# A fixed timetable of seven streams per group, and a residual kept without its mean

## The chip, the cores and the metric

The kernel runs on one core of one Trainium2 chip. The metric is the device time of one execution in microseconds; of several executions the median counts. Five engines work side by side, each through a queue of its own in order: PE (matrix products; PEld is its loading of the stationary operand), DVE and POOL (elementwise work), ACT (functions and copies), and SP, which issues DMAs.

## The reference

128 graphs of 128 nodes with 64 features pass through four layers; each normalises, takes the ReLU, and adds its result to x.

```
h = relu(layernorm(x)); x = x + L0(h, adj)     # 192 hidden values per edge
h = relu(layernorm(x)); x = x + L1(h, adj)     # three graph convolutions, 128 wide
h = relu(layernorm(x)); x = x + L2(h, adj)     # product, row norm, batch norm over all nodes
h = relu(layernorm(x)); x = x + L3(h, adj)     # tanh
L0: mask = adj > 0
    e[j,k] = relu(h[j] @ W1a + (h[j] - h[k]) @ W1b + b1)
    out[j] = sum_k mask[j,k] * e[j,k] @ W2 + deg[j] * b2
L1: three times relu(adj @ (h @ W + b)), then @ Wout + bout, times the node mask
L2: y = ((adj @ h + h) @ W + b); y /= max(|y|, 1e-12)
    mean and variance of y over all nodes of all graphs; relu(affine(y)) * mask
L3: tanh([h, adj @ h] @ W1 + b1) @ W2 + b2
layernorm(x) = (x - mean) / sqrt(var + 1e-5), over the 64 features
```

About one eighth of adj's entries are not zero, so layer 0 need not visit every pair of nodes.

## The kernel before

The 128 graphs form NG = 32 groups of G = 4. Up to the batch norm of layer 2 a group passes through on its own; layer 3 follows for all groups once that norm's mean and variance are known.

**Layer 0 per group.** `prepare` (L406) loads and transposes adj, ranks each node's neighbours with products against triangular matrices (ps_rank, ps_rankT), sorts the nodes by degree (key, lower, ps_place, to_b), and numbers the neighbours (num). It normalises x (layernorm_relu, L316), projects it (ps_q, L468 and L469 copy it) and splits the projection q into three bf16 parts, and it computes the node's own part (ps_p, psort). q and num go to DRAM and come back as near_q and near_n, laid out in thirds of the nodes. A group then has 20 tasks (ORDER, L46): 12 "near" ones and 8 others. For each task ACT fills a PSUM block with psort (`fill`, L563), DVE compares num with a constant to pick one neighbour per node (`make_onehot`, ohn L544 for three tasks at once, oh L549), PE adds the picked q with 4 or 12 matrix products of 128x192 (`differences`, L565), and DVE adds the ReLU of the block to a sum (acc, L582 the first, L586 the others; one per group is made by ACT, L584). There are three blocks, so a block's next fill waits for its accumulation. `layer0_end` (L589) undoes the sort with products (ps_sA, ps_sB), applies W2 and adds to x.

**Layers 1 and 2 per group.** `layer1` (L615) and `layer2_norm` (L648) are chains of product, PSUM copy, product. Every normalisation has on DVE a mean (L303), a subtraction (L304), a sum of squares (L309), a reciprocal (L323) and h (L313), and on ACT a square (L307) and a square root (L321). `layer2_norm` also adds y into column sums that stay in spare PSUM columns (`add_sums`), with the weights as the stationary operand; `total` (L683) picks the own graph's entries and sums.

**What sets the order.** The kernel is recorded group by group. Beside the tasks of group g run two generators, `prepare(g+1)` and `after_layer0(g-1)`. At every half task a budget of estimated PE time (`spent`, PACE, L105 and L748 to L767) decides how many of their steps are recorded. A step often holds several operations of several engines. The framework's scheduler then orders each engine's queue by its own estimates of when operands are ready; it may move instructions against the recorded order.

**The end.** After the last group's layer 2, y loses a first estimate of the mean (shift, L791, made from groups 0 to 29), is squared (L793) and summed. The affine constants follow (L806 to L810). Then the groups pass in parts of 1, 3, 4, 6, 6, 6, 6: `normed` (L833) makes the new x of a group (two operations on POOL, except group 0's, which DVE does; then DVE, with statistics by L845), `roots` (L847) makes the scales of a whole part with a square root on ACT (L857), and `layer3_h`, `layer3_gather`, `layer3_tanh` and `layer3_end` (L865 to L903) make the output. `layer3_gather` brings h into transposed form by a product with the identity (L883).

Of the kernel before, what the change touches and what calls it, by code (L numbers as in the profile page):

```python
# [18 lines left out]
P = 128  # L19
# [28 lines left out]
FIRST, FIRST_R = 0, ORDER.index((None, FULL))  # L48
N_PREPARE, N_AFTER = 14, 26
PACE, LAG = 0.85, 2.5  # L50
LATE = 14
LASTS = 1.9
PARTS = [1, 3, 4, 6, 6, 6, 6]
AHEAD = 3
# [19 lines left out]

def network(ctx, tc, io, out, over=None, x1=None):

    nc = tc.nc  # L80
# [13 lines left out]
    ps = ctx.enter_context(tc.tile_pool(name="ps", bufs=8 - 2 * NBLK, space=PSUM))  # L94

    xs = [keep.tile([P, G, F], F32, tag=f"x{g}", name=f"x{g}") for g in range(NG)]
# [8 lines left out]
    spent = {"us": 0.0, "kind": None}  # L105

    def spend(w, n, dtype):
        f32 = dtype == F32
        kind = (f32, tuple(w.shape), n)
        m = w.shape[-1]  # L110
        one = max(0.026, 0.00043 * n) if not f32 else max(0.22, 0.0018 * n) * (0.5 if m == F and n == P else 1.0)
        spent["us"] += one + (0.045 if kind != spent["kind"] else 0.0)
        spent["kind"] = kind

    def matmul(o, w, x, **kw):
        spend(w, math.prod(x.shape[1:]), x.dtype)
        return nc.tensor.matmul(o, w, x, **kw)  # L117

    def transpose(o, x, i):
        spent["us"] += 0.115  # L120
        spent["kind"] = None
        return nc.tensor.transpose(o, x, i)


    ident = keep.tile([P, P], F32, name="ident")
    make_identity(nc, ident)
    ident_b = keep.tile([P, P], BF16, name="ident_b")
    nc.vector.tensor_copy(ident_b, ident)
# [8 lines left out]
    row = once.tile([P, G, F], F32, tag="db", name="row").rearrange("p b f -> p (b f)")[:, 0:P]  # L137
    nc.gpsimd.iota(row, [[1, P]], base=0, channel_multiplier=0, allow_small_or_imprecise_dtypes=True)
    row_b = keep.tile([P, P], BF16, name="row_b")
    nc.vector.tensor_copy(row_b, row)  # L140
# [21 lines left out]
    nc.gpsimd.memset(order_row, 0.0)  # L162
# [3 lines left out]
    nc.vector.memset(caps[:, 0:1], float(3 * NEAR + FULL))  # L166
    nc.vector.memset(caps[:, 1:2], float(FULL))
    for n in SEGS:
        in_n = work.tile([P, G], F32, tag="mean", name="in_n")[:, 0:1]
        nc.vector.tensor_scalar(in_n, neg_p[:, 0:1], float(-n), float(BLOCKS), ALU.is_gt, ALU.mult)  # L170
        nc.vector.tensor_tensor(caps, caps, in_n.to_broadcast([P, 2]), ALU.add)
# [13 lines left out]
    nc.vector.tensor_scalar(wq, wp, -1.0, None, ALU.mult)  # L185
    nc.vector.tensor_tensor(wp, wp, wtop, ALU.add)
    w2a = keep.tile([P, F], F32, name="w2a")
    nc.sync.dma_start(w2a, w2[0:P, :])
    def blockdiag(name, w, width):

        t = keep.tile([P, 2, width], F32, name=name)
        nc.gpsimd.memset(t, 0.0)
        nc.sync.dma_start(t[0:F, 0, :], w)
        nc.sync.dma_start(t[F:P, 1, :], w)
        return t

    w2b = blockdiag("w2b", w2[P:H0, :], F)
# [14 lines left out]
    gout = load("gout", [P, F], io["L1_gnn_Wout"])  # L212
# [6 lines left out]
    total_n = sum(s.shape[0] for _, ss in parts for s in ss)  # L219
    cat = once.tile([P, NP, W], F32, tag="acc1", name="cat").rearrange("p a n -> p (a n)")[0:3, 0:total_n]  # L220
    where, at = {}, 0
    for name, srcs in parts:
        first = at
        for s in srcs:
            nc.sync.dma_start(cat[:, at : at + s.shape[0]], s.rearrange("(o n) -> o n", o=1).broadcast_to([3, s.shape[0]]))
            at += s.shape[0]
        where[name] = slice(first, at)
    rows3 = keep.tile([P, total_n], BF16, name="rows3")
    nc.gpsimd.memset(rows3, 0.0)

    def split_biases():

        c = ohn.tile([P, 3, G, P], BF16, tag="ohn", name="c3").rearrange("p t b n -> p (t b n)")[0:3, 0:total_n]
        for q in range(3):
            nc.vector.tensor_copy(c, cat)
            if q == 0:
                nc.vector.tensor_scalar(rows3[0:3], c, ident[0:3, 0:1], None, ALU.mult)
            else:
                nc.vector.scalar_tensor_tensor(rows3[0:3], c, ident[0:3, q : q + 1], rows3[0:3], ALU.mult, ALU.add)
            yield  # L240
            if q < 2:
                nc.vector.tensor_tensor(cat, cat, c, ALU.subtract)
                yield

# [11 lines left out]
    b2_all = bias_all("b2_all", io["L0_gnn_b2"])  # L256
# [12 lines left out]
    ysum, ysq = (t.rearrange("p (a n) -> p a n", a=2)[0:G, :, W:512] for t in blks[0:2])  # L269
# [3 lines left out]


    nm_in = once.tile([P, G, P], F32, tag="to", name="nm_in")[:, 0]
    nc.scalar.dma_start(nm_in, nodemask)
    nm = keep.tile([P, P], F32, name="nm")
    pt = ps.tile([P, 512], F32, tag="ps", name="ps_nm")
    transpose(pt[:, 0:P], nm_in, ident)
    nc.vector.tensor_copy(nm, pt[:, 0:P])  # L280

# [10 lines left out]
    def bank(name):  # L292
        return ps.tile([P, 512], F32, tag="ps", name=name)
# [6 lines left out]
    def center(xt, xc, var, tag=""):  # L300

        mean = work.tile([P, G], F32, tag="mean" + tag, name="mean")
        nc.vector.tensor_reduce(mean, xt, AX.X, ALU.add)  # L303
        nc.vector.scalar_tensor_tensor(xc, over_f(mean), -1.0 / F, xt, ALU.mult, ALU.add)  # L304
        yield
        sq = (once if tag else work).tile([P, G, F], F32, tag="sq" + tag, name="sq")
        nc.scalar.activation(sq, xc, AF.Square)  # L307
        yield
        nc.vector.tensor_reduce(var, sq, AX.X, ALU.add)  # L309

# [5 lines left out]
    def layernorm_relu(xt, tag="", h=None):  # L316
        xc = (once if tag else work).tile([P, G, F], F32, tag="xc" + tag, name="xc")
        var = work.tile([P, G], F32, tag="var" + tag, name="var")
        yield from center(xt, xc, var, tag)
# [5 lines left out]
        yield 2  # L325
        return h

    def transposed(h, tag="", pt=None):

        pt = bank("ps_hT") if pt is None else pt  # L330
        for p in range(NP):
            transpose(pt[:, p * P : (p + 1) * P], h[:, 2 * p : 2 * p + 2, :].rearrange("p b f -> p (b f)"), ident)
        hT = (once if tag else work).tile([P, NP, P], F32, tag="hT" + tag, name="hT")
        nc.scalar.copy(flat(hT), pt[:, 0 : NP * P])  # L334
        return hT

    def gathered(h, rT, tag, pt=None):

        pt = bank("ps_ga") if pt is None else pt
        for p in range(NP):  # L340
            for k in range(2):
                b = 2 * p + k
                o = pt[k * F : (k + 1) * F, p * P : (p + 1) * P]
                matmul(o, h[:, b, :], rT[:, b, :], start=True, stop=True)
        t = (once if tag == "hs" else work).tile([P, NP, P], F32, tag=tag, name=tag)
        nc.scalar.copy(flat(t), pt[:, 0 : NP * P])
        return t
# [20 lines left out]
    proj, near_q, near_n = [], [], []  # L368
    for i in range(2 if x1 is None else 0):
        proj.append(keep.tile([P, 3, NP, W], BF16, name=f"q{i}"))  # L370
        near_q.append(keep.tile([P, 3, NP, W], BF16, name=f"near_q{i}"))
        near_n.append(keep.tile([P, 3, G, P], BF16, name=f"near_n{i}"))
        for t in (near_q[-1], near_n[-1]):
            nc.gpsimd.memset(t, 0.0)
# [16 lines left out]
    def save_transposed(g, a):  # L391
        adjT = adjTs[g] = adjp.tile([P, G, P], F32, tag="adjT", name="adjT")
        pt = bank("ps_aT")
        for b in range(G):
            transpose(pt[:, b * P : (b + 1) * P], a[:, b, :], ident)
        nc.scalar.copy(flat(adjT), pt)
        nc.sync.dma_start(saved[g], flat(adjT))
        return adjT

    sorts, psorts, accs = {}, {}, {}  # L400

    def load_group(g):
        nc.sync.dma_start(xs[g], x[g * G : (g + 1) * G].rearrange("b n f -> n b f"))
        loaded[g] = load_adj(g)

    def prepare(g):  # L406

        xt, parts_q = xs[g], proj[g % 2]
# [3 lines left out]

        adjT = save_transposed(g, a)
        mT = once.tile([P, G, P], BF16, tag="mT", name="mT")
        yield
        nc.vector.tensor_scalar(mT, adjT, 0.0, None, ALU.is_gt)
        ln = layernorm_relu(xt, "0")
        next(ln)
        yield
# [4 lines left out]
        pk = bank("ps_rankT")  # L424
        matmul(pk, upto_t, flat(mT), start=True, stop=True)
        leftT = once.tile([P, G, P], BF16, tag="leftT", name="leftT")
        nc.vector.scalar_tensor_tensor(flat(leftT), pk, float(NEAR), flat(mT), ALU.is_gt, ALU.mult)
# [4 lines left out]
        yield  # L432
        pr = bank("ps_rank")
        prv = pr.rearrange("p (b n) -> p b n", n=P)
        for b in range(G):
            matmul(prv[:, b, :], leftT[:, b, :], upto, start=True, stop=True)
        pk = bank("ps_key")
        matmul(pk, ones_b, flat(leftT), start=True, stop=False)
        matmul(pk.rearrange("p (b n) -> p b n", n=P), ones_b, order_row.unsqueeze(1).to_broadcast([P, G, P]), start=False, stop=True)
        key = edge.tile([P, G], F32, tag="key", name="key")  # L440
        nc.vector.tensor_scalar(key, prv[:, :, P - 1], order, None, ALU.add)
        next(ln)
        lower = once.tile([P, G, P], BF16, tag="lower", name="lower")
        nc.vector.tensor_tensor(lower, pk.rearrange("p (b n) -> p b n", n=P), key.unsqueeze(2).to_broadcast([P, G, P]), ALU.is_lt)
        rank = once.tile([P, G, P], BF16, tag="rank", name="rank")
# [645 lines left out]
```

## Time and profile before

| what | us |
|---|---|
| median of 3 runs (1381.01 to 1384.86) | 1383.9 |
| the profiled execution, its time | 1382.45 |
| its span, first to last instruction | 1380.7 |
| PE, DVE, ACT, POOL busy in the span | 1189.1, 1178.6, 986.9, 267.7 |
| accumulations L586, 576 of them | 542.9 on DVE |
| block fills L563, 544 from psort and 96 from psort_r | 436.1 and 78.2 on ACT |
| first and last start of L582, the first accumulation of a group | 45.2 and 1191.7 |

A page of the profile gives each engine's busy time, and groups of equal instructions with their count, busy time, mean time of one in ns, and the idle time of the engine just before them with the instruction that ended most of it. The records name a line, an engine, an operation and the tiles (written <- read). All matrix products of the kernel before carry line 117 or 122, a helper's, so they are told apart by their tiles. "PE blk" is a task's product into a block, whichever task it is. The granted clock of PE is 1.00 in the steady stretch and 0.97 to 0.73 from 1200 to 1300 us.

### The profile page before, as it was taken

How to read it: one execution, taken by the hardware profiler on the slowest of the kernel's cores; microseconds unless marked ns; L12 is line 12 of the kernel's file. 1: busy time of each engine (PE TensorE's matmuls, PEld its weight loads, DVE VectorE, ACT ScalarE, POOL GpSimd, SP SyncE). 2: the span in 40 equal slices, each digit the busy share in tenths (PEclk: the TensorE clock that was granted, in tenths of full speed). 3: DMA queues.
4: the chain of work that ended last, by engine and by line, in shares of the span. 5: the costliest groups of instructions: out<-in, count | busy, mean ns of one | idle time of the engine just before them, and what ended most of it. 6: DMA issues, size and time to landing. Idle time of an engine off the chain costs nothing.

```text
span 1380.7 us, 29280 instructions
## 1 busy us (share of the span) xinstructions
PE 1189.1 (86%) x10968; PEld 961.3 (70%) x10968; DVE 1178.6 (85%) x2643; ACT 986.9 (71%) x1870; POOL 267.7 (19%) x329
## 2 busy tenths in 40 slices
PE   4799888988988888888898988888888888896886
PEld 2577777777777777777777777777777777774665
DVE  7999898889888898898889888889888888874764
ACT  2777777777777777777777777777777777754853
POOL 4111111111111111111111111111111111113652
PEclk8999999999999999999999999999999999998799
DMA  4454222222232232222223333232222222200344
GB/s 119 122 141 113 78 75 67 68 72 84 84 84 84 77 84 73 79 76 72 69 62 84 84 84 85 76 84 76 76 79 72 63 55 71 77 16 15 97 131 107
DMA packets 108787, 110.96 MB, mean 80 GB/s; under 512 B 42895, under 2 KB 88220, under 8 KB 108636
## 3 DMA queue, kind: packets, MB, share of 16 engines
q1 hardware_dynamic: 108172, 108.74, 28.9%
q8 instruction: 88, 1.44, 0.4%
q14 instruction: 63, 0.52, 0.1%
q10 hardware_dynamic: 464, 0.26, 0.1%
HBM read 52.70 MB, written 35.29 MB: 64 GB/s over the span
## 4 chain that ended last, share of the span: by engine, by line
PE 41%; ACT 31%; DVE 20%; issue 4%; DMA 2%; SPq 1%; POOL 0%; DVEq 0%; ACTq 0%
PE blk L117 15%; ACT blk L563 14%; DVE acc L586 8%; PE ps_sA L117 5%; PE ps_pr L117 4%; DVE ohn L544 4%; PE ps_o L117 3%; PE ps_ag L117 3%; ACT extra L528 3%; PE ps_sB L117 3%; PE ps_q L117 2%; ACT q L468 2%; ACT q L470 2%; ACT acc L584 2%; PE ps_hm L117 2%
## 5 line engine op out<-in xcount | busy, mean ns | idle before, releaser
L586 DVE SCALAR_TENSOR_TENSOR acc<-blk,acc 128x768 f32<-128x768 f32 x576 | 542.9, 950 | 92.2 <-PE blk L117 68.4
L563 ACT COPY blk<-psort 128x768 f32<-128x768 f32 x544 | 436.1, 806 | 162.6 <-DVE acc L586 141.5
L117 PE MATMUL blk<-q,oh 128*128 128x192 bf16 x3072 | 324.1, 247 | 28.9 <-ACT blk L563 28.2
L117 PEld LDWEIGHTS <-oh 128*128 128x128 bf16 x3072 | 261.6, 98 | 83.8 <-issue 70.4
L117 PE MATMUL blk<-near_q,ohn 128*128 128x192 bf16 x1536 | 205.5, 247 | 40.8 <-ACT blk L563 28.5
L117 PEld LDWEIGHTS <-ohn 128*128 128x128 bf16 x1536 | 134.4, 98 | 91.3 <-issue 72.9
L544 DVE TENSOR_SCALAR ohn<-near_n 128x1536 bf16<-128x1536 bf16 x128 | 101.9, 838 | 0.0
L471 POOL TENSOR_TENSOR q<-rest,q 128x768 bf16<-128x768 f32 x32 | 52.5, 1642 | 233.9 <-ACT q L470 233.9
L645 POOL TENSOR_TENSOR adjT<-adjT,ident 128x512 f32<-128x512 f32 x32 | 41.8, 1307 | 255.4 <-PE ps_ag L117 255.4
L672 POOL TENSOR_TENSOR y<-y,nrm 128x256 f32<-128x256 f32 x31 | 19.0, 612 | 339.2 <-PE blk L117 305.8
L563 ACT COPY blk<-psort_r 128x768 f32<-128x768 f32 x96 | 78.2, 814 | 0.5 <-DMA fro_r<-fro 0.4
L117 PE MATMUL ps_pr<-g,dT 128*128 128x128 f32 x512 | 71.2, 282 | 5.0 <-ACT dT L629 5.0
L117 PEld LDWEIGHTS ps_pr<-g,dT 128*128 128x128 f32 x512 | 64.5, 191 | 14.0 <-ACT dT L629 13.2
L117 PE MATMUL ps_ag<-adjT,msg 128*128 128x128 f32 x512 | 70.8, 281 | 0.4 <-ACT msg L637 0.4
L117 PEld LDWEIGHTS ps_ag<-adjT,msg 128*128 128x128 f32 x512 | 62.1, 191 | 3.4 <-ACT msg L637 2.8
L629 ACT ACTIVATE dT<-ps_ag 128x512 f32<-128x512 f32 x96 | 56.7, 591 | 6.5 <-PE ps_ag L117 6.5
L117 PE MATMUL ps_q<-wq,hT 128*128 128x384 f32 x128 | 52.2, 531 | 4.6 <-ACT hT L334 0.5
L117 PE MATMUL ps_sA<-fro,acc 128*128 128x128 f32 x256 | 53.3, 290 | 1.3
L637 ACT COPY msg<-ps_pr 128x512 f32<-128x512 f32 x64 | 37.4, 585 | 23.2 <-PE ps_pr L117 23.2
L117 PE MATMUL ps_p<-wp,hs 128*128 128x384 f32 x128 | 51.8, 486 | 0.0
L528 ACT ACTIVATE extra<-psort,spare_n 128x192 f32<-128x192 f32 x128 | 50.4, 453 | 0.1
L117 PE MATMUL ps_sA<-fro_r,acc 128*128 128x128 f32 x256 | 50.1, 277 | 0.0
(226 smaller groups left out, 2493.6 us busy)
## 6 DMA issues: line engine op xcount, KB each, us to landing
q_dram<-q SPq DMA_DIRECT2D x32, 567.0 KB
near_q<-q_dram SPq DMA_DIRECT2D x96, 189.0 KB
near_n<-n_dram SPq DMA_DIRECT2D x96, 126.0 KB
a<-in_adj_dram SPq DMA_DIRECT2D x32, 256.0 KB
adjT_dram<-adjT SPq DMA_DIRECT2D x32, 256.0 KB
adjT<-adjT_dram SPq DMA_DIRECT2D x32, 256.0 KB
psort_r<-psort SPq DMA_DIRECT2D x32, 228.0 KB
fro_r<-fro SPq DMA_DIRECT2D x32, 152.0 KB
```

Of the source, the lines that this page charges most:

```text
L117: return nc.tensor.matmul(o, w, x, **kw)
L468: nc.scalar.copy(parts_q[:, 0, p, :], pq[:, 0:W])
L470: nc.scalar.copy(parts_q[:, 1], rest)
L471: nc.gpsimd.tensor_tensor(parts_q[:, 2], rest, parts_q[:, 1], ALU.subtract)
L528: nc.scalar.activation(of(extra, b), of(psort, b), AF.Relu, scale=spare_n[:, g, b, 0:1])
L544: nc.vector.tensor_scalar(oh.rearrange("p t b n -> p (t b n)"), near_n[g % 2].rearrange("p t b n -> p (t b n)"), float(i + 1), None, ALU.i ...
L563: nc.scalar.copy(columns(t), psorts[g][in_segments(n)])
L584: nc.scalar.activation(acc, o, AF.Relu)
L586: nc.vector.scalar_tensor_tensor(acc, o, 0.0, acc, ALU.max, ALU.add)
L629: nc.scalar.activation(flat(dT), pa, AF.Relu)
L637: nc.scalar.copy(flat(msg), pm)
L645: nc.gpsimd.tensor_tensor(adjT, adjT, ident.unsqueeze(1).to_broadcast([P, G, P]), ALU.add)
```

## The change

All five engines' proxies are wrapped: every instruction that is recorded through them is pinned behind the one recorded before it on its engine. So up to the end stage the recorded order is the order of the queues. The end stage is still left to the scheduler.

```diff
+class InOrder:
+        def call(*args, **kw):
+            ins = op(*args, **kw)
+            if hasattr(ins, "ins"):
+                self.tc.keep_in_program_order(ins)
+            return ins
...
-    nc = tc.nc
+    nc = Engines(tc)
```

The recorded order comes from a timetable. Each group has seven streams: `sort` and `project` (the former prepare), `pick` (one-hots), `fill`, `subtract` (products), `gather` (accumulations) and `after_layer0`. Each is a generator with many short steps, mostly one operation of one engine, and a list of due times, one per step, counted from the group's start; groups start PERIOD = 3491 apart. The step with the earliest due time whose gate is open comes next; a gate asks for a free PSUM bank or for an earlier step. Due times give an order only, nothing on the chip waits for a clock. PSUM banks for side work (2 as before) are now handed out by the kernel. Group 31's streams are paced by 0.75, its last one by 0.4. Group 0 has its tasks in another order, with five that need no near copy first.

```diff
-PACE, LAG = 0.85, 2.5
+ORDERS = {0: OTHERS[:FULL] + [k for k in ORDER if k not in OTHERS[:FULL]]}
+LAST = 0.75, 0.75, 0.4
+PERIOD = 3491
+FILL_PLAN = [-821, -601, -88, -32, 293, 492, 556, 878, 958, 1216, 1216, 1369, ...
+GATHER_PLAN = [-689, -689, -47, 463, 463, 755, 931, 1073, 1306, 1306, 1511, ...
...
+            for stage, plan, start, scale in (
+                (sort, SORT_PLAN, at - PERIOD if g else early, 1.0),
+                (project, PROJECT_PLAN, at - PERIOD if g else early, 1.0),
+                (pick, PICK_PLAN, at, 1.0 if last else LAST[0]),
+                (fill, FILL_PLAN, at, 1.0 if last else LAST[0]),
+                (subtract, SUBTRACT_PLAN, at, 1.0 if last else LAST[0]),
+                (gather, GATHER_PLAN, at, 1.0 if last else LAST[0]),
+                (after_layer0, AFTER_PLAN, at + (PERIOD if last else PERIOD * LAST[0]), (LAST[2], LAST[1], 1.0)[min(last, 2)]),
+            ):
+                streams.append(Stream(stage(g), plan, start, scale))
+        streams.append(Stream(squares(), [0], (NG - 1) * PERIOD))
+        while streams:
+            s = min((s for s in streams if s.gate is None or s.gate()), key=lambda s: s.due())
+            s.step()
```

The residual x is kept without its mean over the features, and the mean in a 65th column. `project` centres x once; what is added later is centred already, since the matrices W2, Wout and the biases b2 and bout are centred during set-up, with their row means in a 65th column. Layers 1 and 2 normalise without a mean and a subtraction. In layer 2 POOL adds the mean back into x.

```diff
-        nc.vector.tensor_reduce(mean, xt, AX.X, ALU.add)
-        nc.vector.scalar_tensor_tensor(xc, over_f(mean), -1.0 / F, xt, ALU.mult, ALU.add)
+    def centre(xm):
+        mean = xm[:, :, F]
+        nc.vector.tensor_reduce(mean, xm[:, :, 0:F], AX.X, ALU.add)
+        yield
+        nc.vector.scalar_tensor_tensor(xm[:, :, 0:F], over_f(mean), -1.0 / F, xm[:, :, 0:F], ALU.mult, ALU.add)
+        nc.vector.tensor_scalar(mean, mean, 1.0 / F, None, ALU.mult)
...
     def layer2_norm(g):
-        h = yield from layernorm_relu(xt)
+        h = yield from norm_relu(xt)
+        nc.gpsimd.tensor_tensor(xt, xt, over_f(xms[g][:, :, F]), ALU.add)
```

The sums of y have y as the stationary operand now, with an eight-column result, and `total` ends in one product. The shift and squares of y become a stream that starts with the last group instead of a loop behind it. In the end stage the transposed h comes from a transpose, and the root of `roots` moves from ACT to POOL.

```diff
-            matmul(sums[:, p, :], weights, t[:, 2 * p : 2 * p + 2, :]..., start=False, stop=True, ...)
+            matmul(sums[:, p, :], t[:, 2 * p : 2 * p + 2, :]..., weights, start=False, stop=True, ...)
...
-            matmul(pt[0:F, n], h[:, b, :], ident, start=True, stop=True)
+            transpose(pt[0:F, n], h[:, b, :], ident)
...
-        nc.scalar.activation(r, r, AF.Sqrt, bias=eps, scale=1.0 / F)
-        nc.vector.reciprocal(r, r)
-        if not late:
+        nc.vector.scalar_tensor_tensor(s0, s1, 1.0 / F, s0, ALU.mult, ALU.add)
+        nc.vector.tensor_scalar(s0, s0, LN_EPS, None, ALU.add)
...
+        if late:
+            nc.gpsimd.tensor_tensor(s0, s0, halves[:, 0 : len(gs), :], ALU.pow)
+            nc.vector.tensor_copy(r, s0)
+        else:
+            nc.gpsimd.tensor_tensor(r, s0, halves[:, 0 : len(gs), :], ALU.pow)
```

In set-up, two casts move from DVE to ACT, the clearing of near_q and near_n from POOL to DVE, the table of capacities from DVE to POOL, and the splitting of the biases is cut in two parts, of which the larger, with the centring of the weights, is a stream of its own.

## The prediction

> **What bounds the kernel now.** I read the windows first. Line L582 runs once per group, at the group's first accumulation, so its starts cut the run: 45.2 us for group 0, 402.1 for group 10, 777.8 for group 20, 1191.7 for group 31. Ten groups in 375.7 us are a period of 37.57 us. The cuts after that are the last accumulation (1222.1), group 31's chain through layers 1 and 2 (to 1262.0), and the final stage. Columns: stretch, its length, busy us (and instructions) of PE, PEld, DVE, ACT, POOL, granted clock, DMA share, GB/s.
>
> ```profile
> 402.10:777.80 375.70, 334.47 (x3093) 273.34 (x3092) 333.89 (x703) 282.00 (x531) 62.04 (x70) 1.00 0.28 77
> 1191.70:1222.10 30.40, 26.61 (x243) 22.68 (x242) 23.27 (x45) 19.07 (x33) 2.62 (x3) 0.94 0.03 10
> 1222.10:1262.00 39.90, 37.65 (x295) 26.13 (x293) 21.33 (x63) 22.64 (x57) 5.88 (x5) 1.00 0.04 14
> 1262.00:1380.70 118.70, 85.47 (x927) 69.12 (x927) 79.15 (x318) 66.80 (x141) 57.42 (x80) 0.84 0.38 99
> ```
>
> In the steady stretch PE and DVE are both 89% busy, and no transfer binds. A busy PE includes pipeline latency: twelve of the 128x192 matmuls take 1.15 us in the timeline, so (1.15 - 0.247)/11 = 0.082 us of PE each, not 0.247. DVE operations overlap by under 0.1 us. So I take DVE as the nearest bound: 33.4 us busy per group, 4.2 idle. Next, what DVE waits for in these ten groups (us in total, times, longest), and the rows of the operations that the change drops:
>
> ```profile
> DVE acc L586 <- PE blk L117: 21.3, 26, 1.8
> DVE rstd L323 <- ACT rstd L321: 10.3, 20, 0.8
> DVE acc L586 <- ACT msg L637: 3.9, 4, 1.0
> DVE acc L586 <- ACT blk L563: 2.6, 3, 0.9
> ```
> ```profile
> L304 DVE SCALAR_TENSOR_TENSOR xc<-mean,x 128x256 f32<-128x256 f32 x30 | 12.5, 416 | 0.2
> L303 DVE TENSOR_REDUCE mean<-x 128x4 f32<-128x256 f32 x30 | 12.3, 410 | 0.0
> ```
>
> Both kinds of wait are of order: a reciprocal placed right behind the square root that feeds it, an accumulation placed ahead of its matmuls. The whole run's chain says the same: it changes engine all the time.
>
> ```profile
> PE 41%; ACT 31%; DVE 20%; issue 4%; DMA 2%; SPq 1%; POOL 0%; DVEq 0%; ACTq 0%
> ```
>
> **Part 1: no mean in the residual.** Before, each of three layer norms per group does mean and subtraction on DVE. After, one norm does, and matrix columns carry the mean on. DVE loses 2 x (410 + 416) = 1.65 us per group and gains one 128x4 scale, 0.16 us by the like-sized row of nrm (L665): -1.5 us. PE's extra columns (260 for 256, 65 for 64) are under 2% of those matmuls. The sums' operands change sides: 128 columns moving become 128 stationary and 4 moving, between 0 and -0.2 us of PE per group; I take 0. POOL gains one addition of the mean per group (736 ns by the row of x<-x,t, L644). POOL is busy 6.2 of 37.6 us, so it hides there unless DVE pays for it. Two notes of the Trainium skill speak against it: "GPSIMD Engine Reference", Engine selection, says two-input elementwise work is about twice as slow there, and Specifications says its SBUF interface is shared with VectorE, in contention with two-port operations or those with two SBUF inputs. The trace agrees on the first (736 ns here, 409 for DVE's x<-x,ps_o) and on the two-port part of the second: min/median/max of one operation, the longest beside POOL's subtraction q<-rest,q.
>
> ```profile
> L544 DVE TENSOR_SCALAR ohn<-near_n x128: 527/553/1816, 43.8 to 1206.2; 128x1536 bf16<-128x1536 bf16 x128
> ```
>
> But accumulations (one SBUF input) take 952 ns beside POOL and 949 without. In the built order DVE's next instructions behind the new addition are rank_t, degs and an accumulation, all reading PSUM. By the rule, with a pick beside it, it costs 32 x 0.74 = 24 us; by the rows and that order, 0. I take 0. The existing collision, 1.26 us per group, I leave: in the new order five accumulations stand between the second rest and the three near picks, and POOL's 1.64 us may fall on either, -1.3 to +0.5 us per group.
>
> **Part 2: the timetable.** The new order puts work between producer and consumer: between var and its reciprocal DVE now has a mean reduction, an accumulation and a near pick (layer 2), a pick and a norm reduction (layer 1), or the group's remaining accumulations and picks (layer 0). Two of three gaps are 1.9 us or more where the longest wait was 0.8, so of 1.03 us per group I take 0.8 away. Removing DVE work that overlapped nothing shortens DVE's own cycle; accumulations are next late, and their 2.1 us behind PE may shrink (matmuls stand further ahead) or grow (PE has less slack: 33.4 of a shorter period). I keep them. Queues that steps pass: SP sends the numbers and their near copies before q, both in use a group later; POOL takes y's product between the two db steps, fed long before. I cost these at nothing; a late near copy would stop PE at the group's boundary, and the DMA wait shown in this stretch is one of 11.1 us, on POOL alone.
> Period: 37.57 - 1.5 - 0.8 = 35.3. Bounds: if PE's waits eat two thirds of it, 36.8; if the accumulations' waits vanish as well, PE's recorded 33.4 is reached, say 34.0. Groups 3 to 30 are 28 periods: 28 x -2.3 = **-64 us** (-100 to -22).
>
> **Part 3: set-up and first groups.** DVE's two casts of constants last 4.8 us each, beside POOL's 2.0 us memsets; upto then starts at 11.1. Now ACT casts, and DVE clears one pair at the start. Group 0 needs no near copy for its first five tasks (before, the first accumulation waited for it, to 45.2). Group 1's preparation, about 8.6 us of DVE before that point, moves behind it. First accumulation near 36 us; group 0 then takes about 29 (before 24.0, with preparation already done), and groups 1 and 2 35.3 each (34.5, 35.6). **-4 us** (-12 to +4): centring the weights adds some 15 small DVE operations of about 0.2 us.
>
> **Part 4: last groups.** Group 31 with its tail to the affine constants is 1191.7 to 1267, 75 us. The chain loses two mean-and-subtract pairs (2 x 0.83 plus two hand-overs of about 0.1 us), and the sums end in one matmul for eight (1.1 us, L686's rows). Squares are no gain by themselves: they still need the mean of group 29, so they start at the last accumulations, and now about 25 subtractions of 0.37 us stand on DVE ahead of group 30's t and group 31's x: 9 us, while before 9.4 us passed from the last accumulation to that x (L613 at 1231.5). Tighter pacing of group 31: 30.4 to about 28. **-6 us** (-14 to +5).
>
> **Part 5: the end.** Columns: group | busy us, mean ns | idle before.
>
> ```profile
> L894 ACT ACT_TABLE_LOAD x6 | 7.7, 1283 | 0.1
> L857 ACT ACT_TABLE_LOAD x5 | 6.4, 1283 | 0.1
> ```
> ```profile
> 1296.62 1.28 ACT L857
> 1297.92 0.32 ACT rstd L857
> 1298.25 1.28 ACT L894
> ```
>
> The second fence is the chain of waits: square root and tanh reload ACT's tables in turn, on the path. Without the root on ACT one load is left; the chain carries 10.9 us of the others. Once the variance (1309.1) waited for a root that ran at 1315.3, queued behind h and hm on ACT, while DVE had only three outputs of 0.42 us to do. In its place POOL raises to a power, at most 24 elements a partition, seven times. No row shows a power; the nearest (128x256 product, 612 to 736 ns) scaled to 24 elements bounds it below at 0.1 us, and I bound it above at 3 us. I take 1.0, the nearer side, since an ordinary addition of ten times the elements costs 0.7. Behind it POOL queues the next part's y, and DVE's less and h wait for it: 7 us. The identity product becomes a transpose: one record of 0.109 us (pitch of ps_aT) for two of 0.054, equal; if it no longer runs beside the adjT product in the other half of the columns, +0.11 x 124 = 14 us of PE, half on the path. I take +1. Sum: -10.9 - 4 + 7 + 1 = **-7 us** (-17 to +10).
>
> **Sum.** -64 - 4 - 6 - 7 = -81. The profiled execution took 1382.45 us (span 1380.7 and 1.75 around it), so it would fall to about 1301.5; it lies 1.45 below the median of the runs shown, 1383.9, and against that median the forecast is **1303**.
>
> **Rivals.** (a) Main case, 55%: 1303, own range 1278 to 1328. (b) DVE's freed time returns as waits for PE, 18%: PE's work hardly falls and PE is as busy as DVE. Period 36.8: -22 - 17 gives 1345. For it: 2.1 us of waits for PE already; against: PE's true pitch. (c) The order closes the accumulation waits too, 15%: period 34.0, -100 - 17 gives 1267. (d) Slower, 10%: ACT's pinned order. Between block fills it holds copies of PSUM results (hT, num, q, ah, fro, dT, msg); if one is not ready, the fill behind it waits, PE waits for the fill, DVE for PE. Its price is the longest like wait, hT behind ps_hT, 1.1 us. The saving of 81 is 2.9 us per period, so three such blocks per group cancel it; with four, 28 x (4.4 - 2.3) - 17 = +42 gives 1426. Against it: ACT is only 75% busy. (e) No change, 2%. That the timetable moves nothing is excluded: all five engines' built orders differ from the first group on.
>
> **Numbers.** A measurement tells about 0.3% (4 us) from no change. Faster (a), (b), (c): 0.88; same 0.02; slower 0.10. The range 1252 to 1352 covers (b) and (c) with the bounds of the power and the start, some 84%; slower is left out.
>
> **What would show it.** First accumulations 35.3 us apart in steady groups; DVE's busy time per group 31.9; its waits for a square root near 0.2 us. One table load behind tanh; the final stage about 112 us; a power's row near 1 us. Wrong if ACT's fills wait for PE copies, if near picks last 1.8 us twice a group, or if the power exceeds 3 us.

## The result, and the profile after

The median went from 1382.45 us (4 runs, 1380.74 to 1384.86) to 1534.88 us (4 runs, 1524.06 to 1540.61): a ratio of 1.109, 95% interval 1.102 to 1.117. The forecast was 1303. The profiled execution took 1529.29 us, with a span of 1527.4. The four runs of the kernel after spread over 16 us, so below, a difference of less than about 10 us is read from the stretches of the traces and not from the totals.

Cut at the same events as before, the span grew in every stretch:

| stretch | before, us | after, us | difference | forecast |
|---|---|---|---|---|
| start to group 3's first accumulation | 139.3 | 163.6 | +24.3 | -4 |
| groups 3 to 30, 28 periods | 1052.4 | 1096.5 | +44.1 | -64 |
| group 31's first accumulation to the root of the affine constants | 73.3 | 94.2 | +20.9 | -6 |
| from there to the end | 115.7 | 173.1 | +57.4 | -7 |

The windows of the kernel after, for ten groups (438.3 to 831.5), group 31 with its tail, and the end; columns as in the prediction:

```profile
438.30:831.50 393.20, 335.07 (x3094) 283.41 (x3093) 317.46 (x671) 284.24 (x530) 70.88 (x80) 0.97 0.27 77
1260.10:1354.30 94.20, 76.74 (x513) 68.20 (x510) 42.03 (x102) 41.80 (x89) 9.40 (x11) 0.75 0.04 10
1354.30:1527.40 173.10, 138.41 (x783) 79.18 (x783) 78.89 (x318) 53.55 (x123) 79.56 (x87) 0.77 0.27 68
```

DVE's work fell to 31.7 us a group, as forecast (31.9), and the period still rose, to 39.2 us on the mean of groups 3 to 30. So idle time grew. The fall of DVE's work is partly luck: by the sums of durations near picks lost 1.26 us a group, which the forecast had left in, and the subtraction of the mean, now beside a cast on POOL, took 0.83 us where 0.42 is usual. The waits in those ten groups (us in total, times, longest), PE's, DVE's and ACT's, and then the last kind as it was before:

```profile
PE blk L90 <- DMA near_q<-q_dram: 19.3, 8, 3.9
DVE acc L90 <- PE blk L90: 56.5, 52, 4.7
ACT zT L90 <- PE ps_ga L90: 20.8, 10, 2.1
ACT msg L90 <- PE ps_pr L90: 12.4, 10, 1.2
ACT rstd L90 <- DVE var L90: 12.0, 20, 0.8
```
```profile
ACT rstd L321 <- DVE var L309: 1.8, 7, 0.3
```

Against before: DVE's 10.3 us behind square roots are gone, and ACT has 12.0 us ahead of them for 1.8; the square root now waits for its input with block fills queued behind it. (Other waits of ACT shrank: those for ps_hT from 10.9 to 2.7 us, those for ps_sB from 10.0 to 2.0.) DVE's waits for PE went from 21.3 to 56.5, and PE waits for a transfer, which it did not. The whole run's chain names the transfers:

```profile
PE 31%; DVE 30%; ACT 14%; DMA 14%; POOL 4%; issue 4%; SPq 2%; DVEq 0%; ACTq 0%; POOLq 0%
```

One boundary between groups in the chain (start us, us, what) shows how:

```profile
626.25 1.66 POOL q L90
627.92 3.36 DMA q_dram<-q
631.30 0.31 SPq L90
...
632.11 4.34 DMA near_q<-q_dram
636.58 1.81 PE blk L90 x20
```

POOL ends q at 627.9, the store lands 3.4 us later, the last near copy at 636.5, and PE's next product in its queue needs that copy. The next group's first accumulation starts at 637.2. Over groups 3 to 30 it starts 9.5 us behind the end of q, before the change 15.3. At such stops the clock falls too: over groups 3 to 30 the mean granted clock is 0.98, before the change 1.00.

### The profile page after: what moved, and what is told of

It reads as the page before. It is cut to its first block, busy times and chain, and to the rows that moved or that the text cites. A ratio compares the mean times of both kernels' runs of the same rounds, so it can differ in the third digit from the quotient of the medians.

```text
span 1527.4 us, 29125 instructions
## 1 busy us (share of the span) xinstructions
PE 1259.2 (82%) x10814; PEld 1022.3 (67%) x10814; DVE 1130.0 (74%) x2575; ACT 981.3 (64%) x1855; POOL 312.3 (20%) x377
## 4 chain that ended last, share of the span: by engine, by line
PE 31%; DVE 30%; ACT 14%; DMA 14%; POOL 4%; issue 4%; SPq 2%; DVEq 0%; ACTq 0%; POOLq 0%
DVE acc L90 14%; PE blk L90 13%; DMA near_q<-q_dram 7%; ACT blk L90 6%; DMA q_dram<-q 6%; PE ps_pr L90 4%; PE ps_end L1071 3%; DVE x L90 3%; POOL q L90 3%; SPq L90 2%; ACT q L90 2%; PE ps_end L1070 2%; PE ps_sB L90 2%; PE ps_ag L90 1%; DVE lower L90 1%
## 5 line engine op out<-in xcount | busy, mean ns | idle before, releaser
L90 PEld LDWEIGHTS <-oh 128*128 128x128 bf16 x3072 | 273.1, 101 | 91.1 <-issue 63.8
L90 PE MATMUL blk<-near_q,ohn 128*128 128x192 bf16 x1536 | 210.9, 253 | 86.2 <-DMA near_q<-q_dram 62.4
L90 DVE SCALAR_TENSOR_TENSOR acc<-blk,extra 128x768 f32<-128x768 f32 x32 | 30.7, 958 | 94.3 <-PE blk L90 94.3
L90 POOL TENSOR_TENSOR x<-x,t 128x260 f32<-128x260 f32 x32 | 24.0, 750 | 367.1 <-DVE t L90 354.1
L90 POOL CAST to<-to_b 128x512 f32<-128x512 bf16 x32 | 32.2, 1006 | 246.1 <-DVE to_b L90 246.1
L90 DVE TENSOR_SCALAR ohn<-near_n 128x1536 bf16<-128x1536 bf16 x128 | 70.6, 553 | 0.2 <-PE blk L90 0.2
L1073 ACT COPY hm<-ps_end 128x512 f32<-128x512 f32 x31 | 18.1, 585 | 81.5 <-PE ps_end L1071 81.5
L1071 PE MATMUL ps_end<-adjT,h 128*64 128x128 f32 x248 | 64.4, 349 | 0.0
L90 ACT COPY msg<-ps_pr 128x512 f32<-128x512 f32 x64 | 37.5, 585 | 40.8 <-PE ps_pr L90 39.3
L90 PE MATMUL ps_q<-wq,hT 128*128 128x384 f32 x128 | 60.2, 553 | 2.2 <-DVE rest L90 0.7
L1070 PE MATMUL ps_end<-ident,h 128*64 128x128 f32 x124 | 41.9, 338 | 23.8 <-ACT h L1062 14.1
```

The source lines that it names most:

```text
L90: ins = op(*args, **kw)
L1070: transpose(pt[0:F, n], h[:, b, :], ident)
L1071: matmul(pt[F:P, n], h[:, b, :], adjT[:, b, :], start=True, stop=True)
L1073: nc.scalar.copy(flat(hm), pt)
```

## The experiments

All times stand beside runs of the kernel before on the same chip (medians of 1382.0 to 1383.6 us); "less" is against the kernel after, 1534.9. "Period" is the mean distance of first accumulations, groups 3 to 30, in the profiled execution. Four stretches are compared: the start (to group 3's first accumulation), the main loop (groups 3 to 30), the tail and the end. The five traces in which the main loop is that of the kernel after (after, e1, e4, e5, e7) have it at 1092 to 1099 us.

**The end: the transpose.** e1 undoes it in the kernel after.

```diff
-            transpose(pt[0:F, n], h[:, b, :], ident)
+            matmul(pt[0:F, n], h[:, b, :], ident, start=True, stop=True)
```

> The kernel after, with the end's transpose of h made a product with the identity again, nothing else. Theory (the transpose takes turns with the adjT product instead of running beside it): in the trace of after a graph costs PE 0.203 + 0.228 + 0.160 = 0.59 us at full clock, against 2 x 0.103 = 0.21 before, and the final stage is 172 us against 114. Undone, 128 graphs give back 128 x 0.38 = 49 us or a little more where the clock is low: about 1485 us (1470 to 1495). Rival (the power on POOL and the waits behind it set the final stage, the transposes only fill time that PE has): within 10 us of 1535.

Measured: 1486.5 us, 48.4 less. The final stage fell from 173.1 to 132.5. e2 makes the opposite edit in the kernel before.

> The kernel before, with only the end's identity product made a transpose. Theory: PE's part of the final stage grows by 49 us, from 85 busy of 119 us, so 15 of them find idle time and 35 to 50 show: 1417 to 1435 us. Rival (the prediction's term of half of 14 us on the path): 1390 us at most.

Measured: 1431.6 us, ratio 1.038 (1.032 to 1.044), 49.6 us more; final stage 166.8 for 115.7. The theory holds both ways. PE's timeline in the kernel after (start, duration, group), then in e1:

```profile
1417.73 0.30 PE L1070 MATMUL ps_end<-ident,h 128*64 128x128 f32 x1
1417.96 0.43 PE L1071 MATMUL ps_end<-adjT,h 128*64 128x128 f32 x2
1418.32 0.30 PE L1070 MATMUL ps_end<-ident,h 128*64 128x128 f32 x1
```

```profile
1430.73 0.27 PE L1070 MATMUL ps_end<-ident,h 128*64 128x128 f32 x1
1430.73 0.27 PE L1071 MATMUL ps_end<-adjT,h 128*64 128x128 f32 x1
1430.84 0.27 PE L1070 MATMUL ps_end<-ident,h 128*64 128x128 f32 x1
1430.84 0.27 PE L1071 MATMUL ps_end<-adjT,h 128*64 128x128 f32 x1
1430.94 0.27 PE L1070 MATMUL ps_end<-ident,h 128*64 128x128 f32 x1
```

In e1 the two products start together, one in each half of the columns, and a graph (two records of each) takes 0.21 us. In the kernel after they start one behind the other, and a graph takes 0.59 us (1417.73 to 1418.32). 128 graphs times 0.38 are 49 us.

**The end: the root.** e7 adds to e1 the square root on ACT and the reciprocal on DVE in place of the power.

```diff
-        nc.gpsimd.tensor_tensor(r, s0, halves[:, 0 : len(gs), :], ALU.pow)
+        nc.scalar.activation(r, r, AF.Sqrt, bias=eps, scale=1.0 / F)
+        nc.vector.reciprocal(r, r)
```

> The kernel after, with the identity product in the end (as in e1_identity_product) and also the roots back on ACT as a square root with a reciprocal on DVE. Theory (seven powers of 1.04 to 4.17 us, 22.9 us together on POOL, stand between a part's statistics and its h; without the transposes nothing hides them, and they cost more than the table loads they save): final stage from 132 to 116 to 122 us, total 1470 to 1477 against 1486.5 for e1. Rival (what the powers cost the table loads cost as well, the rest of the 132 us being the low clock): within 4 us of e1.

Measured: 1470.8 us, 15.7 less than e1; the final stage fell from 132.5 to 114.4, about that of the kernel before (115.7). The powers' rows in the kernel after (min/median/max ns):

```profile
L1042 POOL TENSOR_TENSOR s<-s,halves x3: 4172/4173/4174, 1421.9 to 1484.7; 128x24 f32<-128x24 f32 x3
L1045 POOL TENSOR_TENSOR rstd<-s,halves x4: 1039/2596/4172, 1361.2 to 1398.8; 128x4 f32<-128x4 f32 x1, 128x12 f32<-128x12 f32 x1, 128x16 f32<-128x16 f32 x1, 128x24 f32<-128x24 f32 x1
```

Four elements take 1.04 us and 24 take 4.17. With 2.28 and 2.92 us for 12 and 16 elements in e1's chain, the seven are 22.9 us.

**The tail.** In the kernel after, the square sums of some 24 groups stand on PE in one row ahead of group 31's ps_o. e4 starts that stream later.

```profile
1297.95 22.35 PE L90 MATMUL blk<-nm,sqv 128*128 128x4 f32 x104 [1.29 <-ACT sqv L90]
1320.15 0.78 PE L90 MATMUL ps_o<-w2b,sB 128*128 128x130 f32 x2
```

```diff
-        streams.append(Stream(squares(), [0], (NG - 1) * PERIOD))
+        streams.append(Stream(squares(), [0], (NG - 1) * PERIOD + 3000, 0.5))
```

> The kernel after, with the stream of the squares of y started later and spread, so that group 31's products ps_o stand ahead of most of them on PE. Theory (24 groups' square sums, 96 records of 0.213 us in a row, hold group 31's ps_o for 16.5 us): the tail loses 12 to 17 us, total about 1520 us. Rival (the same PE work in the chain's gaps costs as much there): within 4 us of 1535.

Measured: 1530.1 us; ps_o is added to x at 1298.5 instead of 1323.0, but the tail takes 93.1 us for 94.2, with the clock at 0.50 from 1300 to its end. The theory fails: the place of the sums is not what costs. e5 turns only the sums of the squares round.

```diff
-            add_sums(ysq, nm[:, g * G : (g + 1) * G], sq)
+            add_squares(nm[:, g * G : (g + 1) * G], sq)
...
+    def add_squares(weights, t):
+        for p in range(NP):
+            matmul(ysq[:, p, :], weights, t[:, 2 * p : 2 * p + 2, :].rearrange("p b f -> p (b f)"), start=False, stop=True, skip_group_check=True)
```

> The kernel after, with only the sums of the squares of y turned round again: the weights are the stationary operand and y's square moves with 128 columns, as before. Theory (products with 4 moving columns let the granted clock of PE fall to 0.50 in the tail, and with it everything PE does there takes twice as long): the clock between 1290 and 1340 us is back at 0.9 or more, and group 31's way from its first accumulation to the affine constants falls from 94 to about 78 us, total about 1518 us (1512 to 1524). Rival (the low clock comes from somewhere else, for instance from waits): clock near 0.5 in that stretch and a total within 6 us of 1535.

Measured: 1527.4 us, 7.5 less, which the spread of the runs alone could make. The stretch is clearer: the tail takes 87.2 us, and 87.3 in e12 below, which has the same sums; in the traces of after, e1, e3 and e7, with the sums as in the kernel after, it takes 94.2 to 98.8. That is half of the forecast gain. The clock rose from 0.69 to 0.85 on the mean of 1290 to 1340 us, where 0.9 or more was expected. Windows of 4 us, the last-but-two column is the granted clock; the kernel after, then e5:

```profile
1300.00:1304.00 4.00, 4.00 (x21) 4.00 (x20) 4.00 (x13) 1.99 (x5) 0.00 (x0) 0.50 0.00 0
1304.00:1308.00 4.00, 4.00 (x21) 4.00 (x20) 2.50 (x8) 2.08 (x5) 2.09 (x2) 0.50 0.00 0
1316.00:1320.00 4.00, 4.00 (x21) 4.00 (x20) 0.00 (x0) 2.14 (x6) 0.00 (x0) 0.50 0.00 0
```

```profile
1300.00:1304.00 4.00, 4.00 (x21) 2.15 (x20) 4.00 (x13) 1.87 (x5) 0.00 (x0) 0.50 0.00 0
1304.00:1308.00 4.00, 3.65 (x28) 1.90 (x26) 3.23 (x10) 2.90 (x7) 1.35 (x2) 0.93 0.00 0
1316.00:1320.00 4.00, 2.47 (x22) 1.76 (x21) 2.42 (x8) 1.23 (x4) 0.00 (x0) 1.00 0.00 0
```

In both the clock falls at 1297.8, when PE has been less busy. In e5 it is back after 6.8 us (it falls again at 1331.9); in the kernel after PE is busy for 22 us with 4-column products, 0.213 us apart, and the clock stays at 0.50 until 1328.6. Before the change it was 1.00 from 1222 to 1260. The 14 us by which e5's tail is still longer than before were not traced to one cause.

**The main loop: the boundary.** e3 sets q's steps earlier.

```diff
-PROJECT_PLAN = [..., -57, 1271, 1295, 1481, 1891, 1891, 1990, 2350, 2548, 2548, 2702, 2743, ...
+PROJECT_PLAN = [..., -57, 371, 395, 581, 991, 991, 1090, 1450, 1648, 1648, 1802, 1843, ...
```

> The kernel after, with the steps of the timetable that project, split and store q (transposes of h to the store and its near copies, 11 due times) set 900 earlier, about 9 us. Theory (the group's boundary waits for q's way through DRAM: POOL ends q 9.5 us before the first accumulation, 15.3 us before in the old order, and DVE idles 2.7 us at each boundary): the boundary closes, the period falls from 39.2 to about 36.5, total 1450 to 1475 us. Rival (PE and DVE are held up by other pinned waits, and the boundary's wait comes back elsewhere): period above 38.5 and total above 1510 us.

Measured: 1519.6 us, period 38.7; the main loop takes 1082.7 us for 1096.5. The boundary did close, and the clock is 1.00 in all of the main loop: q ends 15.6 us ahead of the first accumulation, and the time in which PE and DVE are both idle, worked out from the intervals in the trace, falls from 2.3 to 0.2 us a group (2.1 less). But DVE still waits 5.7 us a group (DVE's waits in e3, ten groups, the other rows being small):

```profile
DVE acc L90 <- PE blk L90: 29.7, 47, 1.1
DVE acc L90 <- ACT blk L90: 12.1, 10, 1.2
DVE key L90 <- PE ps_rank L90: 4.7, 10, 0.5
```

The rival was right: other waits took its place. The 1.9 us a group for which PE stopped at near copies were worth 0.5 us a group.

**The main loop: the residual alone.** e8 takes the mean and the subtraction out of two norms of the kernel before.

> The kernel before, whose norms of layers 1 and 2 leave out the mean and its subtraction (that part of the computation is missing, nothing stands in its place): DVE loses 1.65 us of work per group and everything else keeps its order. Theory of the prediction (DVE is the nearest bound, work taken from it shortens the period by as much): period 37.57 - 1.65 = 35.9, total 1382 - 31 x 1.65 = 1331 us (1320 to 1345). Rival (the period is set by hand-overs between PE, ACT and DVE over three blocks, and DVE's freed time becomes idle time): period above 37, total 1360 or more.

Measured: 1308.5 us, ratio 0.946 (0.944 to 0.947), period 35.2. The rival is out, but the gain of 2.3 us a group is more than the 1.65 of the theory: with everything shifted, DVE's instructions meet POOL's at other places. Near picks fell from 3.47 to 2.21 us a group, and picks from num_r rose from 0.84 to 1.48. e9 is the real thing: the kernel before with the 65th column, the centred matrices and POOL's addition of the mean, and nothing else of the change (only the norm of `project` passes xm). Part of its edit:

```diff
-        yield from center(xt, xc, var, tag)
+        yield from center(xc, var, tag, xm)
...
+        if xm is not None:
+            centre(xm)
...
         h = yield from layernorm_relu(xt)
+        nc.gpsimd.tensor_tensor(xt, xt, over_f(xms[g][:, :, F]), ALU.add)
```

> The kernel before with one part of the change alone: the residual is kept without its mean (65th column, centred matrices, the mean added back by POOL in layer 2). Recording, pace and the scheduler's freedom, the sums, the roots and the end stay as before. Theory (this part gives what the prediction said, the timetable took it away): period 35.2 to 35.9, as in e8_no_mean_in_before (35.2, which left the computation out), plus up to 0.5 for POOL's addition of the mean beside DVE; total 1308 to 1330 us. Rival (the addition on POOL, the 65-column forms and the centring of the weights eat the saving): period 37 or more, total 1365 or more.

Measured: **1329.4 us**, ratio 0.961 (0.960 to 0.963), faster than both kernels. Period 35.7. Ten groups of e9 by the windows, its picks of near neighbours, and the last step of its norms, whose two inputs both lie in SBUF:

```profile
389.60:746.40 356.80, 331.06 (x3101) 275.01 (x3102) 312.56 (x642) 283.21 (x533) 68.45 (x80) 1.00 0.29 82
```
```profile
L571 DVE TENSOR_SCALAR ohn<-near_n x128: 524/550/1300, 47.2 to 1153.6; 128x1536 bf16<-128x1536 bf16 x128
L341 DVE SCALAR_TENSOR_TENSOR h<-x,rstd x96: 402/416/1454, 14.3 to 1197.5; 128x256 f32<-128x256 f32 x96
```

DVE is 31.3 us busy a group, 33.4 before. Most picks no longer meet POOL's subtraction q<-rest,q: they sum to 2.2 us a group, before to 3.5. But now one h of each group meets it and takes 1.29 us instead of 0.42. Together the 1.9 us by which the period fell are 1.5 of work, 1.3 of picks, and 0.9 lost on h. So the residual part was forecast rightly in its work, and the loss of the main loop comes from the rest of the change: the timetable with its pins, and what goes with it there (the handing out of PSUM banks, the turned sums of y).

**The main loop: the pinned order.** e6 takes the pins away; the timetable then is only the order of recording.

```diff
-    nc = Engines(tc)
+    nc = tc.nc
```

> The kernel after, with the wrapper that pins each engine's order taken away: the timetable's order is only the order of recording, and the framework's scheduler may move instructions. Theory (the main loop's loss comes from waits that stand in a pinned order, on DVE 7.5 us idle per group against 4.2): the period falls from 39.2 us to 36 to 37.6, total 1535 - 28 x 1.6 to 3.2 = 1445 to 1490 us. Rival (the scheduler's order from this recording waits as much): period 39 or more, total 1525 or more.

Measured: 1461.9 us, 73.0 less, period 37.3, first accumulation at 35.5 us. 49 us of the 73 lie in the main loop (1047.4 for 1096.5) and 19 in the start. To see which queue carries it, one engine at a time was freed, by a line such as `self.tensor = nc.tensor` in the wrapper.

> The kernel after, with only PE's instructions free of the pinned order (the other four engines stay pinned). Theory (most of the loss stands on PE, which waits in its order for q's copies at the boundary, 1.9 us a group, and for side results of DVE, ps_num 1.2 and ps_ga 0.6 us a group): the period falls from 39.2 to 37.5 or less, total 1480 us or less. Rival (it stands on DVE, whose pinned accumulations wait for PE): period above 38.7, total above 1515.

Measured: 1536.0 us, period 39.5. No gain, although PE hardly waits for near copies any more (0.8 us in ten groups): its waits for ACT's fills rise from 11.0 to 33.6 (the kernel after, then e10).

```profile
PE blk L90 <- ACT blk L90: 11.0, 17, 0.9
```
```profile
PE blk L703 <- ACT blk L90: 33.6, 36, 2.0
PE blk L703 <- DMA near_q<-q_dram: 0.8, 1, 0.8
```

> The kernel after, with only DVE's instructions free of the pinned order. Theory that the loss stands on PE: period above 38.5, total above 1510 us. Rival that it stands on DVE: period 37.5 or less, total 1480 us or less. If both orders matter, e10 and this one each give a part of the 73 us that e6_unpinned gave.

Measured: 1507.9 us, period 38.3, 27.0 less; 22 of them in the main loop.

> The kernel after, with only ACT's instructions free of the pinned order. Theory (ACT's pinned order carries the loss: per group it waits 2.1 us for ps_ga, 1.2 for ps_pr and 1.2 for var with block fills queued behind): period 38 us or less, total 1495 or less. Rival (ACT is only late because DVE's accumulations free the blocks late): period above 38.8, total above 1520.

Measured: 1545.3 us, period 39.6: no gain. ACT alone is not the cause.

> The kernel after, with ACT's and DVE's instructions free of the pinned order, PE, POOL and SP pinned. Theory (the fill, product, accumulation ring needs both ends free): period 37.3 as with all five free, total about 1465 (1455 to 1480). Rival (PE's pinned order still holds the ring at near_q and the side products): period above 38, total above 1495.

Measured: 1487.2 us, period 37.7, 47.7 less: between the two expectations. ACT adds nothing alone and 20.7 us once DVE is free. In the main loop alone the two give 42 us, of the 49 that all five give.

> The kernel after, with DVE free of the pinned order and q's steps 900 earlier. Theory (the boundary's wait, 1.9 us a group on PE in both e11_dve_free and after, shows once DVE's own order no longer covers it): period 38.3 - 1.9 = 36.4, total about 1450. Rival (the waits cover each other): period within 0.6 of e11's 38.3, total above 1490.

Measured: 1512.8 us, period 38.7: the rival, no gain over e11.

> The kernel after, with all five engines free and q's steps recorded 900 earlier. If the boundary's wait is part of the 37.3 us of e6_unpinned: period 35.7 to 36.5, total about 1425 (1410 to 1440). If the scheduler places q by itself and the recording doesn't matter: period 37 or more, total 1450 to 1470.

Measured: 1469.1 us, period 37.5: no gain over e6. With free queues the store of q is no cost.

**The sum.** e12 puts the repairs of the end, the sums and q together.

> The kernel after with four edits at once, all tried alone before: identity product in the end, roots back on ACT, squares with y's square moving, q's steps 900 earlier. If their effects add (48.4 + 15.7 + 7.5 + 15.3 = 87 us off 1534.9): about 1448 us (1440 to 1456). If they overlap on the path (a rival cover appears): 1460 or more. Either way what is left above the kernel before, some 65 us, stands in the pinned order of the main loop (38.7 us a group against 37.6) and the tail.

Measured: 1442.7 us, 92.2 less, for a sum of 87: they add, within the spread. Of the 59 us by which its trace is still longer than before, 30 lie in the main loop, 17 in the start and 14 in the tail; the end is 2 shorter.

## Why the prediction was wrong

The trace is 228 us longer than the forecast had it: 108 in the main loop, 64 in the end, 28 in the start and 27 in the tail. Part 2 failed most.

**Part 1, the residual: right in kind and nearly in size.** Alone it gives 53 us (e9), 1.9 us a group where 1.5 was forecast; the work fell as computed. POOL's addition of the mean costs DVE nothing, as forecast: in after and e9 it takes 0.61 us a group, and what DVE does beside it (accumulations 0.95, rank_t 0.68) is as long as elsewhere. What the forecast did not have is that the existing collision moves. In e9 it leaves the near picks and falls on an h with two SBUF inputs (0.42 to 1.29 us), of which kind the prediction had found no row; in the kernel after it falls on the subtraction of the mean (0.42 to 0.83). That the gain on picks and the loss on h partly cancel in e9 is luck.

**Part 2, the timetable: this step failed.** The sum kept DVE's waits for PE ahead of accumulations at 2.1 us a group ("I keep them"; 2.3 with the group's first accumulation). They came to 5.7, most of the 3.9 us by which the period missed its 35.3. Two other sentences stand behind it. First, "I cost these at nothing; a late near copy would stop PE at the group's boundary": it did stop PE, 1.9 us a group, because q is finished 9.5 us ahead of its use where 15.3 had been, and store and reload take 8.7 of them (627.9 to 636.6). The chance was named and not priced, though the built order showed where q stood. Closing it was worth 0.5 us a group (e3). Second, the 0.8 us of square root waits were taken off and nothing put in their place. The consumer moved away from its producer on DVE's queue, but the producer's queue was itself held: ACT now waits 1.2 us a group for those roots' inputs, 2.1 for zT and 1.2 for msg, each with fills queued behind. Against e9, which has the same residual and the old recording, the rest of the change costs 39.2 - 35.7 = 3.5 us a group. Freeing all queues gives 1.9 of it back (e6), ACT's and DVE's alone 1.5 (e14). The other 1.6 is what e6 still has and e9 has not: the timetable as order of recording, the PSUM banks handed out by the kernel, the turned sums of y. Which of these, no run tells. The low clock is not it: it is 1.00 in e6.

**Rival (d), ACT's pinned order, had the right sign and a part of the cause.** e13 shows that ACT alone carries nothing. No one queue carries it all: in the main loop PE alone gives nothing, DVE alone 22 us, DVE with ACT 42, all five 49. In the ring of three blocks, fill on ACT, product on PE and accumulation on DVE, the waits of one engine cover those of another: e3, e15 and e16 closed the boundary's wait and gained 15 us or nothing, and e10 turned it into waits for fills.

**Part 3, the start: wrong.** The first accumulation was put at 36 us and came at 44.6. Of the set-up stream the forecast had the centring, some 15 operations of 0.2 us; these take 4.2 us. Behind them stand the splitting of the biases and some small set-up, which it left out: in all a row of 9.5 us on DVE (timeline of the kernel after, first and last of the row, then the first pick and accumulation):

```profile
30.57 0.20 DVE L90 TENSOR_REDUCE cat<-cat 3x1 f32<-3x64 f32 x1
...
40.09 0.29 DVE L90 COPY nm<-ps_nm 128x128 f32<-128x128 f32 x1
...
41.99 0.28 DVE L90 TENSOR_SCALAR oh<-num 128x512 bf16<-128x512 bf16 x1
44.56 0.96 DVE L90 SCALAR_TENSOR_TENSOR acc<-blk,extra 128x768 f32<-128x768 f32 x1 [2.28 <-PE blk L90]
```

The pins keep it ahead of group 0's picks: with free queues (e6) the first accumulation is at 35.5. The larger part came behind: group 0 took 40.5 us and not 29, groups 1 and 2 39.5 and 39.1 and not 35.3. The granted clock was 0.80 in group 0 and 0.90 in group 1; how much of it is cause and how much effect of the waits, no run tells.

**Part 4, the tail: wrong engine.** The 9 us of subtractions were put on DVE. The cost, as far as it was traced (7 to 12 us of 21), was PE's: sums at half clock. Turned products were costed in the steady stretch alone, "between 0 and -0.2 us", where other products keep the clock up. The Trainium skill ("TensorE: Matmul & The Clock Gate", Part 1) says the clock has a half-rate state which activity lifts within some 4 us. The trace agrees on 0.50 and, with 6.8 us, roughly on the recovery in e5, but 22 us of products in a row did not lift it when each moved 4 columns: here a full row of PE was not enough.

**Part 5, the end: two terms mis-sized.** The transposes were "+1", with +14 x half as the other end; measured about +48. The +0.11 us a graph assumed that a transpose out of the other half's shadow costs one record more. It costs 0.38: neither a transpose nor the products next to it overlap across the change. The Trainium skill had both sides: "Perfetto Trace Analysis", Transposes, advises a transpose over a product, and "TensorEngine Tiling (Array Packing)", Restrictions, says that column tiling excludes transposes with FP32 input. The runs side with the second as far as they go: transposes and products no longer run side by side. That this restriction is the reason, no run shows. The powers were put at 1.0 us each below a bound of 3; they take up to 4.17, and the root's move is a loss of 15.7 us where -8 was forecast. The nearest row was a product, and a power is not like it. The table loads went as forecast, one is left in the end stage (at 1367.6); e7 has ten between square root and tanh again, and is faster than e1 all the same.

## What to carry to other kernels

When a change fixes queues by a timetable, lay each transfer's full way, from the end of its producer to its first use, against the trace's latency before anything else; and count a wait that leaves one engine as moved, until the engine that feeds it is shown to be free. In a ring of engines with few buffers, remove work rather than waits: 2 us less DVE work a group gave 53 us here, while closing 2.1 us of common idle time gave 15. When an order changes, look for where each POOL operation now meets DVE. A transpose is not a free replacement for a product that runs beside another product.

## What the runs showed of the hardware

- An f32 transpose into one column half and f32 products into the other take turns: 0.59 us a graph against 0.21 (e1, e2).
- A power on POOL takes 1.04 us for 4 elements a partition and 4.17 for 24, where a product of 256 elements takes 0.6 to 0.7.
- A row of f32 products with 4 moving columns left the granted clock at 0.50 for 22 us, at 0.213 us each; with the sums turned round it was back after 6.8 us (e5).
- Beside POOL's subtraction q<-rest,q (1.64 us) a DVE operation on two SBUF inputs took 1.29 us instead of 0.42 (h, 29 times in e9), and a bf16 pick up to 1.82 instead of 0.55 (before); accumulations, with one of two inputs in PSUM, kept their 0.95.
